# Small attentions with a written order of issue, layer 2's closing steps moved into the first of them, and a state scan over two states at a time

## The chip, the cores and the metric

The kernel runs on one core of a Trainium2 chip. The metric is the device time of one execution in microseconds (us). It computes a network of four layers over a batch of 16 sequences of 256 tokens with 128 features, all in float32.

The core has five engines that run their own instruction queues side by side, each strictly in order: TensorE (PE: matrix products and transposes, results in PSUM), VectorE (DVE), ScalarE (ACT), GpSimd (POOL) and SyncE (SP, which issues most of the DMAs). A queue whose next instruction waits for another engine holds back everything behind it.

## The reference, cut to what matters

Every layer adds an attention-like result times a gated second result to `x`, and normalises in between:

```python
xn = _layernorm(x)
s = _L2_attn_ref(xn, ...)          # state space scan ("mamba")
g = _silu(_L2_ffn_ref(xn, ...))    # 16 experts, each token takes 2
x = x + s * g
xn = _layernorm(x)
s = _L3_attn_ref(xn, ...)          # 16 heads with a penalty from gates
g = _silu(_L3_ffn_ref(xn, ...))    # two layers: local attention, gated MLP
x = x + s * g
```

The scan in layer 2, for each of 256 inner channels `d` and 16 states `n`, over the tokens of a sequence:

```python
dA = exp(dt_t[..., None] * A)
h = h * dA + (dt_t * u_t)[..., None] * B_t[:, None, :]
y = einsum('bdn,bn->bd', h, C_t)
```

The experts: `h = relu(x @ W1[e] + b1[e]); y = h @ W2[e] + b2[e]`, and a token's result is the sum over its two experts of gate times `y`. The local attention of layer 3: tokens shifted by one in half of the features, `qkv` projection, queries and keys divided by their lengths and rotated, 8 heads with 64 features, windows of 64 tokens that see themselves and the window before, softmax, output projection, added to its input. It is computed twice, each time followed by a gated MLP.

## The kernel before, in words

**Layout.** Tokens are held in 32 tiles of 128 partitions (tokens) by 128 features: `self.x`, the normalised `self.xn`, and `self.xnT`, its transpose. A sequence ("batch" b) is tiles 2b and 2b+1; a "chunk" c is four tiles.

**Layer 2's scan** (`attn2`). Channels lie on partitions (two halves h of 128), tokens in the free dimension, two sequences (512 tokens) to a group, so 8 groups. A step k is one state n of one half h of a group: 32 steps to a group, 256 in all. A step has: `decay` on ACT (`dab`, the exponential, L1122), `states` on DVE (a product `dbb` in PSUM, L1129, then the scan `st`, L1132), `outputs` (the product `hc` with C, L1143, on POOL, in some stretches on DVE) and `sums` on PE (an identity product that adds `hc` over the states into `py`, L1153). `decay` is issued 3 steps ahead, `sums` 3 behind. The rows B and C are loaded for each state, broadcast to all partitions (`bn`, `cn`, 256 KB each, by SP). Within the same steps lies the `prepare` of a later group (projections, convolution by taps, softplus of the step sizes: L1008 to L1086) and the end of an earlier one (`skip` L1159, `times` L1165, `project` L1173, `done` L1184).

**Layer 2's experts** (`ffn2`). After a router, the first 32 steps of the scan also send each token's row twice to a sorted place in DRAM (64 indirect DMAs on POOL, L1328). From step 34 on, 47 blocks of 256 sorted tokens go through their expert's two weights. A block is four "pieces", and `layer2` gives each piece a step by a list (`at`, filled by `later`); before, steps 14 and 15 of each 32 get none. The bias of the second product is one more product (`first` times a `b2` row, L1397). Results go to DRAM, one DMA for each block (L1412).

**Layer 2's end.** After the last piece, `bring` fetches a token tile's two results (2 indirect DMAs on POOL, L1448), `weigh` multiplies by the gates and adds (ACT L1458, DVE L1459), `gated_add` adds silu of that times `s` to `x` (L207 to L209), and `norm_tiles` normalises a chunk: statistics (L168, L169) on DVE, a power on POOL (L158, L159), the normalised tile (L172), transposes and a copy to `xnT` (L194, L195). Each has a step in the list, three quarters of a step per tile; while this runs, `hc` is done on DVE (`alone`). Everything in these steps is chained by `pin`, which fixes the order of issue on each engine to the order of the program.

**Layer 3.** `layer3` loads the weights, computes `gates3` (64 products with one column, L1485, two powers on POOL, L1490 and L1495, a transpose), then runs `local_attention`, `gated_mlp`, both again, and the last attention. `local_attention` is a pipeline written out by hand over i from -3 to 16, in which five batches are in different stages: `begin` (transposes, L1708, and copies to `hT`), `turned` (projection L1717, square on ACT L1730, length sums L1731, rotation L1732, L1735 on DVE, L1740 on POOL), `values` (L1747), `lengths` (reciprocal roots on DVE, L1664 to L1674, scaled keys L1760), `across` (transposes L1767), `scores` (mask L1778, products L1787, maxima L1797, exponentials L1806, shares L1814 and L1815), `keys_first` (L1825), `weigh` (L1839) and `finish` (L1855, L1862). It isn't pinned: a scheduler that orders instructions before the program is built may move them past each other.

Of the kernel before, what the change touches and what calls it, by code (L numbers as in the profile page):

```python
# [19 lines left out]
P = 128  # L20
B = 16
# [52 lines left out]
class Net:  # L74
# [756 lines left out]
    def layer2(self, ydram, consts):  # L831
# [10 lines left out]
        with ExitStack() as ctx:  # L842
            fin = ctx.enter_context(self.tc.tile_pool(name="l2_f", bufs=2))
# [18 lines left out]
            experts = self.ffn2(ctx, consts["experts"])  # L862


            k = SENT + 1
            later(k, experts["begin"])
            for i in range(experts["pieces"]):
                k += 1
                while k % 32 in (14, 15):
                    k += 1  # L870
# [3 lines left out]
            fetch = self.fetch = k + 2  # L874
            for t in range(NT):
                k = fetch + 3 * t // 4
                later(k, lambda t=t: experts["bring"](t))
                later(k + 3, lambda t=t: experts["weigh"](t, f))
                if t % 4 == 3:
                    c = t // 4  # L880
                    k = max(k + 4, STEPS + 11 if c == 7 else 0)
                    later(k, lambda c=c: self.gated_add(fin, 4 * c, chunk(f, c), 4))
                    later(k + 1, lambda c=c: self.norm_tiles(fin, psa, c, "pa"))

            mark = len(nc.cur_bb.bb.instructions)
            for k in range(max(at) + 1):
# [3 lines left out]
                scan["step"](k, k < SENT or k >= fetch)  # L890
                for f_ in at.get(k, ()):
                    f_()
            self.pin(mark)

# [15 lines left out]
    def layer2_constants(self, cp):  # L910
# [12 lines left out]

        first = cp.tile([P, P], F32, name="first")
        nc.gpsimd.memset(first, 0.0)
        nc.gpsimd.memset(first[0:1, :], 1.0)
# [17 lines left out]
        return {"scan": scan, "experts": (wr, br, b1, step, row, first)}  # L944

    def attn2(self, ctx, psa, consts, later):
# [12 lines left out]
        AHEAD, BEHIND = 3, 3  # L959
# [4 lines left out]
        dap, stp, hcp = enter("a2_da", AHEAD + 2), enter("a2_st", 3), enter("a2_hc", BEHIND + 2)  # L964
        bc = enter("a2_b", 4)
        dram = enter("a2_d", 2, space=DRAM)
        psd = enter("a2_db", 1, space=PSUM)
        psy = enter("a2_py", 1, space=PSUM)
# [7 lines left out]
        state = {}  # L976

        def prepare(gr, base):
# [109 lines left out]
            def broadcast(n):  # L1088
                for i, name in ((8, "bn"), (24, "cn")):
                    d[name, n] = self.load(  # L1090
                        bc, d["dr"][i + n, :].partition_broadcast(P), name, shape=[P, T]
                    )
# [54 lines left out]
        def sums(k):  # L1147
# [3 lines left out]
            if n == 0:  # L1151
                d["py", h] = psy.tile([P, T], F32, name=f"py{h}")
# [33 lines left out]
        def step(k, alone):  # L1186
# [7 lines left out]
            elif k == STEPS:  # L1194
                outputs(k - 1, None)
# [797 lines left out]
```

## Time and profile before

| what | value |
|---|---|
| median of 3 runs | 3000.88 us (2999.2 to 3001.28) |
| the profiled execution's own time | 3015.23 us |
| its span, first to last instruction | 3013.5 us |
| busy: PE, DVE, ACT, POOL | 2490.4, 2033.4, 1523.9, 1352.7 us |
| mean granted TensorE clock | 0.884 |

The span can be cut into stages by the first and last start of their lines: the scan's steps run from 874.0 (first L1129) to 1596.9 (last L1132), the sends from 910.6 to about 997, the experts from about 1014 to 1519, the fetches from 1524.6, the first small attention from about 1666 to 2026, the second to 2498, and the last attention to the end. "Busy" is the time in which an engine had at least one instruction running. PE's matrix products are pipelined and their ends are modelled, so that its busy share overstates it; for PE, times from one start to the next are the safer measure. Idle time of an engine that isn't the bottleneck costs nothing.

### The profile page before, as it was taken

How to read it: one execution, taken by the hardware profiler on the slowest of the kernel's cores; microseconds unless marked ns; L12 is line 12 of the kernel's file. 1: busy time of each engine (PE TensorE's matmuls, PEld its weight loads, DVE VectorE, ACT ScalarE, POOL GpSimd, SP SyncE). 2: the span in 40 equal slices, each digit the busy share in tenths (PEclk: the TensorE clock that was granted, in tenths of full speed). 3: DMA queues.
4: the chain of work that ended last, by engine and by line, in shares of the span. 5: the costliest groups of instructions: out<-in, count | busy, mean ns of one | idle time of the engine just before them, and what ended most of it. 6: DMA issues, size and time to landing. Idle time of an engine off the chain costs nothing.

```text
span 3013.5 us, 48937 instructions
## 1 busy us (share of the span) xinstructions
PE 2490.4 (83%) x17715; PEld 1618.9 (54%) x17743; DVE 2033.4 (67%) x4222; ACT 1523.9 (51%) x3371; POOL 1352.7 (45%) x1185
## 2 busy tenths in 40 slices
PE   5999983779666699999944699988799998789988
PEld 3666572556431366666613366665366665555555
DVE  4666423335488688888885678854678864478885
ACT  1555460213244466667641367771267774465564
POOL 2000002113237566665665545541355554288886
PEclk8999985779876799999975799998899999899998
DMA  2110002000113466666631000000100000112110
GB/s 64 29 30 26 8 4 100 1 15 15 43 46 120 132 186 178 181 180 179 183 100 53 14 14 13 16 8 0 39 15 12 15 12 4 36 39 45 31 47 8
DMA packets 155195, 168.94 MB, mean 56 GB/s; under 512 B 22817, under 2 KB 102874, under 8 KB 154954
## 3 DMA queue, kind: packets, MB, share of 16 engines
q1 hardware_dynamic: 146378, 147.71, 17.8%
q0 software_dynamic: 6496, 17.05, 1.7%
q8 instruction: 141, 2.31, 0.3%
q10 hardware_dynamic: 2080, 1.05, 0.1%
q14 instruction: 100, 0.82, 0.1%
HBM read 127.57 MB, written 29.79 MB: 52 GB/s over the span
## 4 chain that ended last, share of the span: by engine, by line
PE 27%; DVE 23%; POOL 8%; ACT 8%; issue 4%; DMA 2%; SPq 1%; another core or an unknown queue 0%; DVEq 0%; POOLq 0%; ACTq 0%
PE py L1153 5%; ACT p L1806 3%; POOL e L313 3%; DVE st L1132 2%; DVE rot L1732 2%; DVE ss L1731 2%; DVE sn L1735 2%; PE py L1399 2%; PE ph L1373 2%; DVE nm L1797 2%; PE ps L1787 2%; PE ph L1927 2%; PE pa L1008 1%; PE pa L325 1%; PE ph L1931 1%
## 5 line engine op out<-in xcount | busy, mean ns | idle before, releaser
L346 DVE TENSOR_REDUCE nmax<-pa 128x2 f32<-128x512 f32 x512 | 329.5, 683 | 142.4 <-PE pb L335 112.6
L335 PE MATMUL pb<-qa,kT 32*128 32x256 f32 x2048 | 387.3, 422 | 26.5 <-ACT e L356 26.5
L356 ACT ACTIVATE e<-pb 128x512 f32<-128x512 f32 x512 | 286.2, 594 | 228.4 <-PE pb L335 207.2
L325 PE MATMUL pa<-kT,qT 32*128 32x256 f32 x2048 | 367.1, 435 | 19.2 <-DMA kT<-qkd 17.7
L1143 POOL TENSOR_TENSOR hc<-st,cn 128x512 f32<-128x512 f32 x207 | 264.2, 1278 | 208.0 <-DVE dbb L1129 91.6
L1153 PE MATMUL py<-hc,ident 128*128 128x512 f32 x512 | 298.1, 674 | 65.6 <-DVE hc L1143 32.0
L1132 DVE TENSOR_TENSOR_SCAN st<-dab,dbb 128x512 f32<-128x512 f32 x256 | 312.5, 1221 | 34.1 <-ACT dab L1122 4.5
L325 PEld LDWEIGHTS pa<-kT,qT 32*128 32x128 f32 x2048 | 232.7, 200 | 103.3 <-issue 55.4
L335 PEld LDWEIGHTS pb<-qa,kT 32*128 32x128 f32 x2048 | 249.7, 195 | 55.4 <-ACT e L356 47.0
L1122 ACT ACTIVATE dab<-dl,A_log 128x512 f32<-128x512 f32 x256 | 181.3, 719 | 147.7 <-DVE st L1132 105.6
L313 POOL TENSOR_TENSOR e<-e,pen 128x1024 f32<-128x1024 f32 x96 | 228.9, 2395 | 59.1 <-ACT e L356 58.3
L1806 ACT ACTIVATE p<-ps,nm,rl 128x128 f32<-128x128 f32 x512 | 227.8, 466 | 29.8 <-DVE nm L1799 29.0
L1815 POOL TENSOR_TENSOR p<-p,den 128x512 f32<-128x512 f32 x128 | 133.0, 1041 | 231.4 <-DVE den L1814 225.8
L158 POOL TENSOR_SCALAR ln_r<-ln_mv 128x4 f32<-128x4 f32 x32 | 7.4, 232 | 495.3 <-DVE ln_st L168 419.4
L1717 PE MATMUL pm<-wqkv,hT 128*128 128x512 f32 x384 | 209.9, 661 | 17.7 <-DVE hT L1711 8.4
L1740 POOL TENSOR_TENSOR rot<-rot,sn 128x512 f32<-128x512 f32 x128 | 162.6, 1270 | 108.5 <-DVE sn L1735 61.9
L1129 DVE TENSOR_TENSOR dbb<-du,bn 128x512 f32<-128x512 f32 x256 | 202.9, 793 | 6.6 <-DMA bn<-dr 0.6
L1153 PEld LDWEIGHTS py<-hc,ident 128*128 128x128 f32 x512 | 95.2, 210 | 169.4 <-issue 76.8
L1730 ACT ACTIVATE sq<-pm 128x512 f32<-128x512 f32 x128 | 75.1, 618 | 136.2 <-PE pm L1717 136.2
L1787 PE MATMUL ps<-kT,qT 64*64 64x128 f32 x2048 | 136.1, 287 | 0.0
L382 PE MATMUL pm<-e,vaug 128*32 128x256 f32 x2048 | 128.9, 394 | 3.1 <-DVE s L416 3.1
L1787 PEld LDWEIGHTS ps<-kT,qT 64*64 64x64 f32 x2048 | 90.4, 136 | 72.1 <-issue 69.3
(375 smaller groups left out, 5614.2 us busy)
## 6 DMA issues: line engine op xcount, KB each, us to landing
bn<-dr SPq DMA_DIRECT2D x128, 256.0 KB
cn<-dr SPq DMA_DIRECT2D x128, 256.0 KB
w<-in_L_ffn_W_dram SPq DMA_DIRECT2D x94, 256.0 KB
qkd<-qk SPq DMA_DIRECT2D x32, 256.0 KB
v<-v SPq DMA_DIRECT2D x64, 128.0 KB
f_y<-y SPq DMA_DIRECT2D x47, 128.0 KB
f_x<-zero POOLq DMA_DIRECT2D x8, 704.0 KB
xr<-f_x SPq DMA_DIRECT2D x44, 128.0 KB
```

The costliest lines, as they stand in the source:

```text
L313: eng.tensor_mul(pairs[m], pairs[m], pen.to_broadcast([P, 2, 2, S]))
L325: nc.tensor.matmul(pa[:, t, :], qbuf[b % 4][r : r + 32, g, ts], kbuf[b % 4][r : r + 32, g, :], start=True, stop=True,)
L335: nc.tensor.matmul(pb[:, t, :], kbuf[b % 4][r : r + 32, g, ts], qas[m // 8][r : r + 32, g % 2, :], start=True, stop=True,)
L346: nc.vector.tensor_reduce(nbuf[n // 8 % 2][:, :, u // 4, u % 4, 8], pa, AX.X, ALU.max, negate=True)
L356: nc.scalar.activation(e, pb, AF.Exp, scale=scale)
L1129: mul = nc.vector.tensor_mul(db, d["du"][:, h, :], d["bn", n])
L1132: nc.vector.tensor_tensor_scan(d["st", r], d.pop(("da", r)), db, 0.0, ALU.mult, ALU.add)
L1143: ins = eng.tensor_mul(d["hc", r], d.pop(("st", r)), d["cn", r // 2])
L1153: nc.tensor.matmul(d["py", h], self.ident, d.pop(("hc", r)), start=(n == 0), stop=(n == N - 1))
L1717: nc.tensor.matmul(pj, hTs[b % 3][:, t * P : (t + 1) * P], d["qkv"][:, j * 512 : (j + 1) * 512], start=True, stop=True,)
L1787: nc.tensor.matmul(ps[i][64 * half : 64 * half + 64, c, w, :], qT[f, 2 * u + c, q0 : q0 + 64], kT[f, 2 * u + c, keys[half] : keys[half] + ...
L1806: nc.scalar.activation(p[:, c, w, :], ps[i][:, c, w, :], AF.Exp, scale=r[:, w, 0, h + 2 * c : h + 2 * c + 1], bias=nm[:, c, w : w + 1], ac ...
```

## The change

1. **The scan takes two states at a time.** `dab`, `dbb`, `st`, `hc`, `bn` and `cn` become tiles of 128 by 2 by 512. The multiply, the scan and the product each run once per pair of steps over 1024 elements; the exponential (its scale differs by state) and the sum on PE stay single. The first token of a sequence has its step size set to 1e28, so that a scan starts afresh there, and two states can lie end to end. Rings: `dab` 3 pairs, `st` 2, `hc` 3, `bn` and `cn` 2 (before: 5, 3, 5, 4 single). `decay` is 4 steps ahead, `sums` 5 behind. `dbb` takes two PSUM banks.
2. **Experts.** The bias of the second product moves out of the blocks: the gates' transpose `gT` and eight products with the biases (`spread`, `biases`, `biased`, in the first 32 steps) fill `f` beforehand, and `weigh` adds both results to it on DVE. Hidden results have one PSUM bank instead of two; transposes and second results share another. Six of each 32 steps get no piece before step 224, and from there on none is left out, which puts the last piece at step 261 (before: 237).
3. **Layer 2's end** leaves the pinned steps. `layer2` returns a function `end(n)`, which for tile n brings, for tile n-1 weighs, and for a chunk adds, takes statistics, or normalises. `local_attention` calls it seven times before its loop and twice in each round in its first run; its transposes in `begin` also fill `xnT`.
4. **Order of issue of `local_attention`.** `turned`, `values`, `scores`, `begin` and `finish` are split into their parts on PE, ACT, DVE and POOL, placed one by one in the loop, and the loop is pinned. Copies to `hT` and of the values move from DVE to ACT.
5. **`gates3`** comes after the first `local_attention`.

```diff
+            later(1, experts["spread"])
+            for c in range(NT // 4):
+                k = (4, 7, 16, 19, 22, 25, 28, 31)[c]
+                later(k, lambda c=c: experts["biases"](psa, c))
+                later(k + 1, lambda c=c: experts["biased"](c))
...
-                while k % 32 in (14, 15):
+                while k < STEPS - 32 and k % 32 in (5, 9, 12, 14, 15, 19):
...
+        def end(pool, n):
+            if 0 <= n < NT:
+                experts["bring"](pool, n)
+            if 0 <= n - 1 < NT:
+                experts["weigh"](n - 1)
+            c, r = divmod(n - 5, 4)
+            if 0 <= c < NT // 4 and r == 0:
+                self.gated_add(fin, 4 * c, chunk(f, c), 4)
+            if 0 <= c < NT // 4 and r == 1:
+                stats(c)
+            if 0 <= c < NT // 4 and r == 2:
+                normed(c)
...
-        AHEAD, BEHIND = 3, 3
+        AHEAD, BEHIND = 4, 5
...
-        dap, stp, hcp = enter("a2_da", AHEAD + 2), enter("a2_st", 3), enter("a2_hc", BEHIND + 2)
-        bc = enter("a2_b", 4)
+        dap, stp, hcp = enter("a2_da", 3), enter("a2_st", 2), enter("a2_hc", 3)
+        bc = enter("a2_b", 2)
...
-            db = psd.tile([P, T], F32, name="dbb")
-            mul = nc.vector.tensor_mul(db, d["du"][:, h, :], d["bn", n])
-            outputs(k - 1, mul)
-            d["st", r] = stp.tile([P, T], F32, name="st")
-            nc.vector.tensor_tensor_scan(d["st", r], d.pop(("da", r)), db, 0.0, ALU.mult, ALU.add)
+            db = banks["db"].tile([P, 2, T], F32, name="dbb")
+            du = d["du"][:, h, :].rearrange("p (o t) -> p o t", o=1).to_broadcast([P, 2, T])
+            mul = nc.vector.tensor_mul(db, du, d["bn", n])
+            outputs(k - 2, mul)
+            d["st", r] = stp.tile([P, 2, T], F32, name="st")
+            wide = lambda t: t.rearrange("p o t -> p (o t)")
+            nc.vector.tensor_tensor_scan(
+                wide(d["st", r]), wide(d.pop(("da", r))), wide(db), 0.0, ALU.mult, ALU.add
+            )
...
-            nc.tensor.matmul(py[:, q, :], first, b2s[j % 3], start=True, stop=False)
...
-        def weigh(t, f):
-            g0, g1 = (got.pop(("rows", t, k)) for k in range(K))
-            nc.scalar.activation(f[:, t, :], g0, AF.Copy, scale=gate[:, 0, t : t + 1])
-            nc.vector.scalar_tensor_tensor(
-                f[:, t, :], g1, gate[:, 1, t : t + 1], f[:, t, :], ALU.mult, ALU.add
-            )
+        def weigh(t):
+            for k in range(K):
+                nc.vector.scalar_tensor_tensor(
+                    f[:, t, :], got.pop(("rows", t, k)), gate[:, k, t : t + 1], f[:, t, :],
+                    ALU.mult, ALU.add,
+                )
...
                     if l == 0:
+                        with tc.tile_pool(name="l2_g", bufs=3) as got:
+                            self.local_attention(X, d, lambda n: end(got, n))
                         g, dr = self.gates3(gp, dram)
-                    self.local_attention(X, d)
+                    else:
+                        self.local_attention(X, d)
...
-                hT = hTs[b % 3]
-                nc.vector.tensor_copy(hT[0:64, :], pt[0:64, :])
-                nc.vector.tensor_copy(hT[64:128, 1:S], pt[64:128, 0 : S - 1])
+            def begun(b):
+                pt, hT = rows[b].pop("pt"), hTs[b % 3]
+                nc.scalar.copy(hT[0:64, :], pt[0:64, :])
+                nc.scalar.copy(hT[64:128, 1:S], pt[64:128, 0 : S - 1])
+                if end is not None:
+                    nc.scalar.copy(self.xnT[:, b * S : (b + 1) * S], pt)
...
+            mark = len(nc.cur_bb.bb.instructions)
+            if end is not None:
+                for n in range(7):
+                    end(n)
             for i in range(-3, B + 1):
                 run(scores, i, 0)
-                run(turned, i + 2, 0, 0)
-                run(turned, i + 2, 0, 1)
-                run(keys_first, i - 1, 2)
+                run(times, i + 2, 0, 0)
+                run(squares, i + 2, 0, 0)
+                run(powers, i, 0, 0)
+                run(times, i + 2, 0, 1)
+                run(squares, i + 2, 0, 1)
+                run(turned, i + 2, 0, 0)
+                run(keys_first, i - 1, 2)
+                run(powers, i, 0, 1)
+                run(shares, i, 0, 0)
+                run(turned, i + 2, 0, 1)
                 run(keys_first, i - 1, 3)
+                run(shares, i, 0, 1)
...
+                if end is not None:
+                    end(2 * i + 13)
                 run(scores, i, 1)
...
+                if end is not None:
+                    end(2 * i + 14)
+                run(begin, i + 3)
+                run(begun, i + 3)
                 run(weigh, i, 1)
-                run(begin, i + 3)
+            self.pin(mark)
```

## The prediction

> **What bounds the kernel now.** I read the table of stretches first, having cut the span at the places where the code changes stage. Its columns are the stretch, its length, then busy time (and instructions) of PE, PEld, DVE, ACT and POOL, granted clock, DMA share and GB/s.
>
> ```profile
> 1014.00:1519.00 505.00, 479.20 (x2115) 311.45 (x2114) 443.76 (x438) 337.33 (x605) 306.81 (x241) 0.98 0.61 176
> 1519.00:1673.00 154.00, 59.07 (x158) 33.50 (x159) 95.11 (x220) 38.68 (x71) 94.75 (x92) 0.61 0.23 66
> 1673.00:2022.00 349.00, 317.25 (x2787) 206.40 (x2800) 268.38 (x734) 238.02 (x764) 178.41 (x163) 0.95 0.06 13
> 2022.00:2141.00 119.00, 98.30 (x465) 64.90 (x462) 53.41 (x148) 19.53 (x30) 23.37 (x32) 0.84 0.02 7
> 2157.00:2500.00 343.00, 314.43 (x2829) 207.85 (x2840) 257.63 (x708) 238.22 (x765) 174.85 (x160) 0.96 0.06 13
> ```
>
> In order: scan with experts, layer 2's end, first small attention, its gated layer, second small attention. The scan has two full engines (PE 479 and DVE 444 of 505). Layer 2's end has none: PE is busy for 59 of 154 us. In the attentions PE is busy for nine tenths.
>
> Next the timeline of the scan, and three single rows (start, duration, engine, line, operation).
>
> ```profile
> 1512.71 1.22 DVE L1132 TENSOR_TENSOR_SCAN st<-dab,dbb 128x512 f32<-128x512 f32 x1
> 1512.72 1.27 POOL L1143 TENSOR_TENSOR hc<-st,cn 128x512 f32<-128x512 f32 x1 [0.83 <-DVE dbb L1129]
> 1513.96 0.70 DVE L1129 TENSOR_TENSOR dbb<-du,bn 128x512 f32<-128x512 f32 x1
> ...
> 1499.86 1.27 POOL L1165 TENSOR_TENSOR xz<-xz 128x512 f32<-128x512 f32 x1
> 1499.88 1.80 DVE L1129 TENSOR_TENSOR dbb<-du,bn 128x512 f32<-128x512 f32 x1
> ...
> 887.41 2.28 DVE L719 TENSOR_TENSOR_SCAN f_run<-ones,f_num 128x1024 f32<-128x1024 f32 x1
> 898.14 1.22 DVE L1275 TENSOR_TENSOR f_run<-f_run,f_num 128x1024 f32<-128x1024 f32 x1
> ```
>
> A step is multiply, a gap of 0.12, scan: 2.09 us. Twice the width costs 2.28 and 1.22, not 2.44 and 1.40. A multiply beside a POOL operation grows to 1.80.
>
> Last, layer 2's end (timeline and chain of waits) and the steady attention (waits: total, times, longest).
>
> ```profile
> 1602.18 1.14 POOL L1448 DMA_INDIRECT got<-f_y,slot  x1 [0.19 <-issue]
> 1603.63 0.96 POOL L1448 DMA_INDIRECT got<-f_y,slot  x1 [0.30 <-issue]
> ...
> 1618.46 2.11 DVE L208 TENSOR_TENSOR gate<-gate,s 128x512 f32<-128x512 f32 x1 [0.70 <-ACT gate L207]
> ...
> 1635.28 10.37 PE pc L1485 x48
> 1658.97 5.44 POOL g L1490
> 1666.99 5.45 POOL reach L1495
> ...
> PE ps L1778 <- DVE rl_t L1673: 9.7, 10, 1.0
> ```
>
> 64 gathers go one by one on POOL, about 1.26 us apart, and every chunk of four tiles passes gather, addition, layernorm, transpose before the next moves on; then come the gates. The attention's first work on DVE (L1731) starts at 1673.65. From there PE repeats every 20.38 us (L1855 at 1864.86 and 1885.24), with waits of 1.0 us and some 0.4 in small ones: 18.9 us of PE per batch.
>
> **The Trainium skill.** (1) "VectorE: DVE Perf Modes", section on the TRN2 errata: a fp32 tensor_tensor takes (N+151)/0.96 ns, so the fixed part is paid once per instruction; 512 gives 691, 1024 gives 1224. The trace agrees (0.70 and 1.22). (2) "SBUF — State Buffer", "SBUF: two separate sides": a DVE operation with two SBUF inputs and a GpSimd operation take a lock, and the later one waits for the whole of the other. The 1.80 above and the 2.11 of L208 (0.69 elsewhere) agree. (3) "ScalarE: Activation LUTs", "What ACT_TABLE_LOAD costs": 1283 ns and a drain of 1380. The trace has the 1283; at 1541.73 the next activation followed after 1.29, so I take 1.28 and keep 2.66 as the upper end.
>
> **The change, part by part.**
>
> *Scan in pairs.* Per pair DVE runs one multiply (1.22), the gap (0.12) and one scan (2.28). POOL's product, 128x1024, takes 2.35 (L1078's row) and starts with the scan, so it ends some 0.1 after it, and the next multiply must wait for that: 3.75 per pair, 1.88 per step against 2.09. Each group of 32 steps adds 5.6 us of DVE (L1070, L1081, L1159 twice, L1184): 0.18 per step; waiting for other POOL work makes the mean multiply 0.825 instead of 0.70: 0.12. DVE falls from 2.39 to 2.18 per step, to 0.91.
> PE per step before: the sum 0.86 (start to start in the timeline); experts 30 pieces in 32 steps, four to a block, a block being hidden 2×0.87, result 2×0.90, bias 2×0.22, transposes 0.44: 1.04; a group's preparation and projection, 14×0.86 plus 2.3, over 32: 0.45. Sum 2.35, of 2.51 measured (175 scans in 440 us). After: bias matmuls gone, 26 pieces in 32: 0.86+0.81+0.45 = 2.12, to 0.90. The 32 steps from 224 have a piece each and no preparation: 1.91.
> I take both down together: 2.51×0.907 = 2.28. Where does it start? The 64 sends on POOL end at 997 and the experts' tokens wait for them, so a faster start of the scan waits at step 32: nothing gained before 1014 (step 38). Then 186×2.28 + 32×2.04 + 6 steps of pieces alone at an estimated 1.5 = 498: the last result is stored at 1512, with the scan finished; before it was 1519 with 16 steps left. ACT rises to about 1.8 per step, still under 2.28. Broadcast loads halve in number and double in size, issued five steps ahead; eight bias loads replace 47 on SP; nothing waits there. Tighter buffers (two state pairs, one bank for hidden) bound the pace: 2.13 if none shows, 2.51 if they eat the gain.
>
> *Layer 2's end.* Before: 1519 to 1673.65, 154.6 us. After, what must precede the attention: store to first gather 5.4 (as 1519.14 to 1524.57), 14 gathers of seven tiles 17.6 (addition and statistics of chunk 0 run beneath them), POOL's power 1.3, normalising 1.3, transposes, copies, projection and square 3.2: 28.8. L1731's successor starts at 1541, 132.6 earlier. The layer's weights load on SP behind the last store, under these 29 us (before, SP issued them in 10.6, from 1648.86 to 1659.44); if late they cost up to 5.
>
> *First attention.* What was moved lands here, per batch (two tiles): DVE +3.2 (four weighings at 0.3, half an addition 0.7, statistics 0.8, normalising 0.5), minus the value and hT copies 2.2, plus 0.5 for locks: 16.8 becomes 18.3. ACT 14.7 + 2.2 for those copies, xnT and silu + 1.3 table loads: 18.2 (19.6 with the drain). POOL 11.0 + four gathers 5.0 + 0.65: 16.7. All are under PE's 18.9 but close, and order of issue is fixed: a weighing that waits for its gather holds up DVE's score maxima behind it, which ACT's exponentials and then PE wait for. A gather has half a batch (10 us) of lead over its use, on a POOL with 4 us free. I take 20.9 per batch (19.3 to 23): +8 over 16.
>
> *Gates.* They now stand between attention and gated layer, and the order shows them in PE, DVE and POOL ahead of its first chunk: 64 products 12.2, power 5.4, power 5.4 partly beside statistics: +22 (15 to 26). In the old place they were part of the 154.6.
>
> *Second attention.* No moved work; DVE 15, ACT 16.6; the fixed order can at most close PE's 1.5 us of waits per batch. I take half, 19.7: −11 (19.0 to 20.6).
>
> Sum: −132.6 + 8 + 22 − 11 = −114 against the profiled execution's 3015.2 (span 3013.5, 1.7 around it), which ran 0.5% above the median 3000.9. Predicted median: 2888.
>
> **Rivals.** *The scan keeps 2.5 per step*: a POOL extra (2.9 us for L1084, 2.5 for two L1165) delays the product, two state pairs give only the multiply's 1.2 us of slack, and DVE stops. For it: 307 of 505 us on POOL and locks both ways. Against: PE and DVE both lose a tenth. +58: 2946. *Everything closes up*: 2.13 per step (−28), 19.3 and 19.0 per batch (−26, −11): 2823. For it: no engine's load exceeds these; against: four engines over 85%. *Slower*: gathers on POOL fall behind products and additions, DVE waits at each weighing, twice per batch, and a fixed order lets nothing pass. It decides from 20.4+(114+8)/16 = 28 us per batch, which is 3.5 us of wait at each weighing beyond my 20.9; at 30 the time is 3034. Against: POOL has 4 us to spare per batch. *The pin repeats what the scheduler did*: second attention unchanged, 2899; inside my case.
>
> **How the numbers follow.** Mine 62%, scan unchanged 16%, all closes 14%, slower 4%, other losses that stay faster 3%, a tie 1%. Range 2830 to 2948: from near the closed case to just over the unchanged scan. What this measurement can tell from no change is 0.2%, 6 us: faster 0.95, same 0.01, slower 0.04.
>
> **What would show it.** Scans of 2.28 every 4.5 us; last store near 1512; first L1803 within 30 us of it; batches of 20 to 21 us, then 19 to 20; 20 us of PE near idle after the first attention. A first attention over 25 us per batch, or scan pairs of 5 us, would make it wrong.

## The result, and the profile after

| | before | after |
|---|---|---|
| median of 11 runs on the same chips | 3000.47 us (2994.54 to 3002.32) | 2976.30 us (2966.43 to 2988.81) |
| ratio, 95% interval | | 0.9923 [0.9904, 0.9941] |
| the profiled execution | 3015.23 us | 2966.91 us |

The change makes the kernel faster by 24 us, well outside 0.2%. The forecast was 2888, and 2976 lies above its range. The two profiled executions differ by 48 us, since the one before ran 15 us above its median and the one after 9 below its own. The eleven runs after spread over 22 us, and the shortest has the higher mean granted clock (0.897, against 0.889 in the longest). The stages below are cut from profiles and add up to 48, not 24.

The table of stretches of the kernel after, cut at its own stages: scan with experts, layer 2's start-up before the attention, first small attention, gates with the first gated layer, second small attention. Columns as before: stretch, length, busy time of PE, PEld, DVE, ACT, POOL, granted clock, DMA share, GB/s.

```profile
1014.00:1522.00 508.00, 464.25 (x1941) 289.03 (x1939) 436.38 (x250) 335.69 (x607) 310.11 (x146) 0.99 0.57 179
1522.00:1551.00 29.00, 4.74 (x21) 3.13 (x20) 11.31 (x39) 3.41 (x7) 19.46 (x25) 0.62 0.42 123
1551.00:1955.00 404.00, 317.27 (x2848) 206.61 (x2847) 314.17 (x819) 284.60 (x865) 234.91 (x221) 0.89 0.08 19
1955.00:2086.00 131.00, 103.58 (x478) 71.06 (x478) 53.94 (x154) 17.73 (x25) 34.50 (x38) 0.79 0.00 1
2086.00:2454.00 368.00, 292.08 (x2852) 192.81 (x2851) 254.93 (x681) 258.32 (x833) 178.04 (x162) 0.96 0.08 19
```

The 154 us in which no engine was full have become 29. But the first attention, with the same 317 us of PE as before, takes 404 instead of 349 us, and DVE has gone from 268 to 314 us in it.

| stage, us | before | forecast | after |
|---|---|---|---|
| last expert result stored at | 1519.1 | 1512 | 1522.4 |
| from there to the attention's first work on DVE (L1731, L1803) | 154.6 | 29 | 29.2 |
| first small attention, to its last sum into `X` | 352.7 | 361 | 403.4 |
| gates (now here) and first gated layer | 111.3 | 133 | 131.3 |
| second small attention | 360.5 | 350 | 367.3 |
| the rest | 515.3 | 515 | 511.7 |

A steady batch is the distance between two sums into `X`: 20.4 us before in both attentions; after, 24.1 and 23.7 in turn (mean 23.9) in the first and 20.9 in the second.

Who waits for whom. First the list of waits of DVE in the first attention of the kernel after (1640 to 1850), then the list of PE's and DVE's waits in its second (2150 to 2370); columns: waiting line, what ended the wait, us in total, times, longest.

```profile
DVE gate L208 <- ACT gate L207: 17.0, 5, 4.6
DVE nm L1867 <- PE ps L1858: 5.8, 5, 1.4
```

```profile
DVE nm L1867 <- PE ps L1858: 41.8, 21, 3.9
PEld po L1916 <- ACT oT L1926: 27.0, 21, 1.7
PE po L1916 <- ACT oT L1926: 16.1, 21, 0.9
```

In the second attention DVE is early: it waits 42 us in 220 for scores. In the first that reserve is gone. What used it up is in the groups of DVE in the first attention (count, busy us and mean ns, idle before):

```profile
L1518 DVE SCALAR_TENSOR_TENSOR xnT<-got,gates,xnT 128x128 f32<-128x128 f32 x30 | 22.1, 736 | 0.5
L904 DVE TENSOR_SCALAR xn<-x,ln_mv,ln_r 128x128 f32<-128x128 f32 x16 | 7.3, 516 | 0.0
L208 DVE TENSOR_TENSOR gate<-gate,s 128x512 f32<-128x512 f32 x5 | 3.5, 692 | 17.0 <-ACT gate L207 17.0
```

A weighing costs 736 ns on the mean where the shortest of the 64 takes 320, and each product with the gate has 3.4 us of idle DVE ahead of it. One such place, from the timelines of ACT and of DVE:

```profile
1734.44 0.37 ACT L1926 COPY oT<-po 128x256 f32<-128x256 f32 x1 [0.28 <-PE po L1916]
1734.83 1.28 ACT L207 ACT_TABLE_LOAD   x1
1736.12 0.63 ACT L207 ACTIVATE gate<-xnT 128x512 f32<-128x512 f32 x1
...
1739.08 1.28 ACT L1881 ACT_TABLE_LOAD   x1 [1.42 <-DVE nm L1869]
```

```profile
1732.08 1.62 DVE L1518 SCALAR_TENSOR_TENSOR xnT<-got,gates,xnT 128x128 f32<-128x128 f32 x2
1736.78 0.69 DVE L208 TENSOR_TENSOR gate<-gate,s 128x512 f32<-128x512 f32 x1 [3.09 <-ACT gate L207]
```

ACT issues the silu behind its copies, the last of which has waited for PE, and must load a table for it; DVE stands at L208 for 3.1 us, with the maxima (L1867) queued behind it, and ACT's exponentials then wait 1.4 us for those maxima. It looks like a complete story: a wait that the fixed order passes on. The experiments show that it is only a part.

### The profile page after: what moved, and what is told of

Its sections match the earlier page's. It is cut to its first block, busy times and chain, and to the rows that moved or that the text cites. A ratio compares the mean times of both kernels' runs of the same rounds, so it can differ in the third digit from the quotient of the medians.

```text
span 2965.2 us, 47535 instructions
## 1 busy us (share of the span) xinstructions
PE 2391.3 (81%) x17543; PEld 1561.1 (53%) x17543; DVE 1984.8 (67%) x3841; ACT 1559.5 (53%) x3490; POOL 1360.3 (46%) x1084
## 3 DMA queue, kind: packets, MB, share of 16 engines
q8 instruction: 139, 2.28, 0.3%
## 4 chain that ended last, share of the span: by engine, by line
PE 24%; DVE 15%; ACT 14%; POOL 8%; issue 3%; DMA 3%; SPq 1%; POOLq 0%; DVEq 0%; ACTq 0%
ACT p L1881 6%; PE py L1192 3%; POOL e L313 3%; DVE nm L1867 2%; PE ps L1858 2%; PE ph L2035 2%; ACT pT L1907 1%; PE po L1916 1%; PE ph L1435 1%; PE pa L1037 1%; PE ph L2039 1%; PE pa L325 1%; PE py L2051 1%; DMA xr<-f_x 1%; PE pb L335 1%
## 5 line engine op out<-in xcount | busy, mean ns | idle before, releaser
L1182 POOL TENSOR_TENSOR hc<-st,cn 128x1024 f32<-128x1024 f32 x111 | 261.2, 2353 | 194.6 <-DVE dbb L1165 117.1
L1169 DVE TENSOR_TENSOR_SCAN st<-dab,dbb 128x1024 f32<-128x1024 f32 x128 | 292.7, 2287 | 24.5 <-ACT dab L1155 9.1
L1192 PE MATMUL py<-hc,ident 128*128 128x512 f32 x512 | 267.7, 613 | 10.3 <-DVE hc L1182 8.7
L1165 DVE TENSOR_TENSOR dbb<-du,bn 128x1024 f32<-128x1024 f32 x128 | 188.8, 1475 | 5.0 <-DMA bn<-dr 2.4
L1867 DVE TENSOR_REDUCE nm<-ps 128x4 f32<-128x512 f32 x128 | 87.6, 684 | 107.8 <-PE ps L1858 106.5
L1916 PE MATMUL po<-pT,v 128*64 128x64 f32 (+1 forms) x1536 | 95.3, 265 | 64.2 <-ACT oT L1926 49.6
L1916 PEld LDWEIGHTS po<-pT,v 128*64 128x64 f32 x1536 | 76.5, 150 | 109.6 <-ACT oT L1926 83.0
```

The lines of the kernel that those rows point to most:

```text
L1165: mul = nc.vector.tensor_mul(db, du, d["bn", n])
L1169: nc.vector.tensor_tensor_scan(wide(d["st", r]), wide(d.pop(("da", r))), wide(db), 0.0, ALU.mult, ALU.add)
L1182: ins = eng.tensor_mul(d["hc", r], d.pop(("st", r)), d["cn", r // 4 * 2])
L1192: nc.tensor.matmul(d["py", h], self.ident, d["hc", r - r % 2][:, r % 2, :], start=(n == 0), stop=(n == N - 1))
L1916: nc.tensor.matmul(po[64 * i : 64 * i + 64, P * w + q0 : P * w + q0 + n], v[:, k, hs], pT[:, i, w, q0 : q0 + n], start=True, stop=True, ti ...
```

## The experiments

The stages of all runs, in us, as in the table above (start-up, first attention, gates and gated layer, second attention), and the ratio to the kernel before on the same chip:

| run | start-up | first | gated | second | ratio [95%] |
|---|---|---|---|---|---|
| before | 154.6 | 352.7 | 111.3 | 360.5 | 1 |
| after | 29.2 | 403.4 | 131.3 | 367.3 | 0.9923 [0.9904, 0.9941] |
| e_split | 30.3 | 422.9 | 133.5 | 371.3 | 0.9994 [0.9981, 1.0007] |
| e_copy | 29.8 | 401.1 | 131.3 | 375.1 | 0.9924 [0.9899, 0.9949] |
| e_nopin | 42.8 | 393.8 | 130.5 | 350.7 | 0.9864 [0.9827, 0.9901] |
| e_old1 | 29.3 | 409.3 | 131.3 | 360.2 | 0.9874 [0.9847, 0.9900] |
| e_endfirst | 111.4 | 366.6 | 133.0 | 370.7 | one run |
| e_chunkfirst | 30.1 | 372.8 | 130.7 | 367.9 | one run |
| e_nogather | 9.7 | 405.1 | 131.3 | 378.3 | one run |
| e_anchor | 29.2 | 436.0 | 130.8 | 351.1 | 0.9974 [0.9959, 0.9988] |
| e_slots | 33.1 | 399.3 | 130.6 | 378.4 | 0.9861 [0.9829, 0.9892] |
| e_best | 33.3 | 394.1 | 130.7 | 351.1 | 0.9815 [0.9795, 0.9835] |
| e_best_gates | 33.0 | 396.9 | 111.2 | 371.5 | 0.9794 [0.9763, 0.9826] |
| e_scan | 33.1 | 398.0 | 130.6 | 350.9 | 0.9798 [0.9773, 0.9823] |
| e_final | 35.7 | 424.0 | 131.3 | 350.8 | 0.9905 [0.9882, 0.9929] |
| e_act | 33.0 | 414.8 | 130.6 | 350.9 | 0.9912 [0.9879, 0.9945] |

### The gate in two pieces (e_split)

```diff
             if 0 <= c < NT // 4 and r == 0:
-                self.gated_add(fin, 4 * c, chunk(f, c), 4)
+                at["gate", c] = g = fin.tile([P, 4, D], F32, name="gate")
+                nc.scalar.activation(g, chunk(f, c), AF.Silu)
             if 0 <= c < NT // 4 and r == 1:
+                ...  # product, sum into x
                 stats(c)
```

> Layer 2's gate in two pieces: silu in the place where the whole gated addition stood, product and sum one call of end() later (half a batch), beside the statistics. Both table loads stay. First theory (DVE stands in fixed order behind a silu that ACT issues only after the copies of oT, 3.1 to 4.6 us each time, 8 times): the rounds with a chunk's addition fall from 26.4 to about 22.5 us, the first attention from 403 to about 372, the whole by 25 to 35. Rival (ACT's two table loads of 1.28 us are the cost, wherever DVE stands): ACT is late for the exponentials all the same, the first attention stays above 393. Rival (any fixed order costs this): stays at 403.

The wait at the gate is gone, and the first attention is 20 us longer: rounds of 24.5 and 26.6. My first theory fell. Product, sum and statistics now form one lump of DVE work at the start of a round. From 1640 to 1850, PE's products wait 19.8 us, in five times, for DVE (L1842, released by `den`, L1898). That the lump costs more than the wait did is a likely reading; no run takes the two apart.

### No table loads (e_copy)

```diff
             if 0 <= c < NT // 4 and r == 0:
-                self.gated_add(fin, 4 * c, chunk(f, c), 4)
+                ...
+                nc.scalar.copy(g, chunk(f, c))
+                ...  # product, sum into x
```

> silu left out of layer 2's closing addition (a plain copy in its place), so that no table is loaded within the first attention; the order is that of the changed kernel, so DVE still waits for ACT's copy behind the copies of oT. First theory (DVE's place in the order): DVE's wait falls only by the load, from 3.1-4.6 to 1.8-3.3 us, and the exponentials' own reload of 1.28 goes too: 8 x 1.3 to 2.6 = 10 to 21 us less, first attention at 382 to 393. Rival (table loads are the cost): rounds with an addition come down to the 21.4 us of the others, first attention at 363 to 370.

The silu is left out, and a plain copy stands in its place. 401.1 against 403.4: fourteen table loads of 1.28 us, 18 us of ACT (68 loads in the kernel after, 54 here), were worth about 2 us. Neither theory's number came. DVE still stood ahead of the product, 12.3 us in five times.

### No chain (e_nopin), and the old second attention (e_old1)

```diff
-            self.pin(mark)
```

> local_attention without its chain (pin), everything else as in the changed kernel: the scheduler may move instructions past each other in both small attentions. Theory of the fixed order (it costs 7 us in the second attention and part of the 44 in the first): the second attention goes from 363 back to about 356 or below, the first to below 385. Rival (the moved work costs the same whoever orders it; the written order is no worse): the second stays at 360 to 366 and the first at 395 to 410, or grows where the scheduler hoists gated additions ahead of the maxima.

> The second small attention alone in the form of the kernel before (no chain, copies to hT and of the values on DVE), the first as in the changed kernel. If the written order or the copies on ACT cost the second attention its 7 us: it goes from 362.7 to 354-358 and the whole falls by about 7. If the 7 us came from what lies around it (its weights, the clock): it stays at 360-366.

Both second attentions are shorter than the chained one. With the pieces and the copies on ACT, but no chain, it takes 350.7, with rounds of 20.4 and last rounds of 16.2, 13.2 and 8.4 where the chain had 20.8, 20.3 and 10.1. The old form gives 360.2, as before. So the pieces gain about 10 us and the chain loses 17 or more, most of it in the last three rounds (51 us for 38). Within the steady rounds, what goes is PE's wait for the single `po` bank: 16.1 us in 220 with the chain for the products (the 27.0 of the weight loads run in part at the same time and don't add to it). In the second attention of the run without the chain, the products' largest wait is another, and the weight loads' wait for the bank is small:

```profile
PE ps L1849 <- ACT p L1881: 12.7, 11, 1.2
PEld po L1916 <- ACT oT L1926: 4.7, 11, 0.4
```

In the first attention the scheduler drew fetches and additions forward: three rounds of 33.4, 29.3 and 29.2, then 20.4 in the rest. Start-up and attention together take 436.6, against 432.6 with the chain: not faster there, only in the second attention.

### Which part of the moved work (e_endfirst, e_chunkfirst, e_nogather)

```diff
# e_endfirst
-                for n in range(7):
+                for n in range(NT + 8):
                     end(n)
...
-                if end is not None:
-                    end(2 * i + 13)
...
-                if end is not None:
-                    end(2 * i + 14)
# e_chunkfirst: gated_add, stats, normed of all chunks ahead of the loop
# e_nogather: the weighings read one constant tile
-                nc.gpsimd.indirect_dma_start(...)
+                gk = xs_
```

> All of layer 2's end (64 fetches, weighings, additions, statistics, normalising) ahead of the first attention's loop, none within it; the loop's chain is unchanged. If the moved work makes the loop's rounds longer (23.9 us per batch): they fall to the second attention's 20.9, the first attention to about 360, and the stretch from the last store to the attention's first work on DVE grows from 29 to about 95 (50 more fetches at 1.26 and the last chunk's end). Rival (the chain, or the copies to xnT, or the clock after a long idle stretch, make the first attention slow by themselves): rounds stay above 22.5.

> Additions, statistics and normalising of all chunks run ahead of the loop, on what f holds then (so the values are others: the fetched rows come too late for them); fetches and weighings stay in the loop. It cuts the moved work in two. Theory A (DVE's and ACT's part of a chunk: silu, product, sum, statistics, normalising, about 2.2 us of DVE per batch): rounds fall from 23.9 to 21 to 21.7. Theory B (fetches on POOL, the weighings behind them and their locks): they stay at 23 to 23.9. Both in part: about 22.4.

> The 64 fetches left out: the weighings read one constant tile, so that POOL has 5 us less per batch and no weighing waits for a transfer or a fetch's lock; all of DVE's and ACT's work stays in its place. Theory A (DVE's and ACT's part): rounds stay at 23 to 23.9. Theory B (fetches): they fall to 21 to 21.7. The stretch before the attention falls from 29 to about 12 either way.

These three agree, each in a single run. With nothing moved into it, the loop runs at 20.9 to 22.4, mostly 20.9. Without additions, statistics and normalising: 21.4, 21.4, 22.0 in turn, mean 21.6. Without the fetches: 23.7 to 24.2 as in the kernel after, once the first rounds are past. In the rounds whose granted clock is 1.00 throughout, the three stand at 20.9, 21.4 and 24.1. So of the 3 us per batch, some 2.3 to 2.7 belong to the work that is done once per chunk on DVE and ACT, 0.5 to 0.7 to weighings with fetches, and the fetches on POOL cost nothing that shows. (In e_chunkfirst the scheduler drew seven of the eight chunks' additions forward into the scan, whose last store moved to 1539.9; its loop is what counts here.) DVE's waits for the maxima, in e_chunkfirst (1640 to 1800) and in e_nogather (1640 to 1830):

```profile
DVE nm L1867 <- PE ps L1858: 17.6, 7, 3.0
```

```profile
DVE gate L208 <- ACT gate L207: 14.6, 4, 4.6
DVE nm L1864 <- PE ps L1855: 5.3, 4, 1.9
```

Without the chunk's work part of DVE's reserve is back; without the fetches it isn't.

### Held in place without a chain (e_anchor)

Each instruction of `end` is tied behind the one ahead of it on its engine; the attention's own are free.

> No chain over the loop; only the instructions of layer 2's end are held behind the instruction ahead of them on their engine in the program, so that the scheduler orders the attention's own work freely but can't draw the moved work forward, as it did in the run without a chain (33, 29, 29 us in the first three rounds). If the chain's 0.5 us per round and its slow end (12 us) are the attention's own and the moved work costs 3 us per batch wherever it is spread: second attention 351 as without a chain, first about 385, the whole at 2940 to 2955. Rival (the moved work's cost grows again without the chain): first attention at 394 or more, the whole not under 2960.

The rival was right, and more than right: 436.0, with rounds of 26 to 31. What makes it worse was not taken apart. The second attention, where nothing is tied, takes 351.1 again.

### Other places for the moved work (e_slots), and a free second attention (e_best)

```diff
...
+            elif part == "mid":          # ahead of the middle maxima
+                c, r = divmod(i + 3, 2)
+                if r == 0 and c < NT // 4:
+                    normed(c)
+                if r == 1 and c + 1 < NT // 4:
+                    added(c + 1)         # product, sum, statistics
+                for t in (12, 13):
+                    weigh(2 * i + t)
+                bring(2 * i + 14)
+            else:                        # end of the round
+                ...
+                    silu(c)              # half a round before its product
+                bring(2 * i + 15)
...
# e_best besides
-            self.pin(mark)
+            if end is not None:
+                self.pin(mark)
```

> Layer 2's moved work takes other places in the same chain. In the undisturbed rounds DVE waits for scores twice: 3.9 us ahead of the maxima in the middle of a round, 0.3 ahead of those at its start. All of DVE's moved work (both weighings, product, sum, statistics, normalising: about 3.6 us per batch) goes ahead of the middle maxima; the silu is issued half a round before its product, so that DVE never waits for it. If the place decides (one us of DVE ahead of the early maxima lengthens the round by one us, ahead of the middle ones by nothing until 3.9 are used): rounds fall from 23.9 to 21 to 21.6, the first attention to 368-378, the whole from 2976 to about 2945-2955. Rival (DVE's amount decides, wherever it stands): rounds stay at 23 or more, the first attention over 395.

> As the run with the moved work ahead of the middle maxima, and the chain only in the first small attention: the second is left to the scheduler, with the pieces as they are. Expected: both gains add, first attention 368-378, second 351 in place of 367, the whole 2928 to 2940. Rival: the second attention without a chain was fast only because the first had none either: stays at 360 or more.

The place helps far less than I expected, and the rival was the nearer: rounds of 24.1 and 22.3, a mean of 23.2 for 23.9, and a first attention of 399.3. In e_best the second part held: 351.1 in the second attention, and 0.9815 [0.9795, 0.9835] in all. Why the place gave so little can be read in e_best. All the weighings there cost 346 ns, but now the first operation in the slot pays. The group of the four normalisings between 1756 and 1761 (min/median/max), and POOL's timeline beside it:

```profile
L904 DVE TENSOR_SCALAR xn<-x,ln_mv,ln_r x4: 335/338/2571, 1756.7 to 1759.7; 128x128 f32<-128x128 f32 x4
```

```profile
1755.91 1.05 POOL L1922 TENSOR_TENSOR p<-p,den 128x512 f32<-128x512 f32 x1
1756.91 1.27 POOL L1839 TENSOR_TENSOR rot<-rot,sn 128x512 f32<-128x512 f32 x1
1758.13 1.04 POOL L1922 TENSOR_TENSOR p<-p,den 128x512 f32<-128x512 f32 x1
```

The first normalising starts at 1756.7 and ends only when POOL's last product does, at 1759.2: 2.57 us for 0.34. In the same place product and sum cost 1.50 and 1.41 instead of 0.69. This fits the lock that the Trainium skill, page "SBUF — State Buffer", section "SBUF: two separate sides", describes: it is taken for a whole instruction. The attention's large DVE operations that read an operand from PSUM keep their time (L1804: 0.68 us on the mean in both attentions); the work that was moved in has all its operands in SBUF, and met the lock in both arrangements.

An estimate from the means and shortest times: weighings and normalisings lose 2.0 us per batch in the kernel after (4 x 0.42 + 2 x 0.18), and normalisings, product and sum 2.1 in e_best (2 x 0.65 + 0.77). So these waits did not go, they moved to other operations. With them, DVE is busy for 191.06 of the 210 us from 1640 to 1850 in e_best, or 21.1 us of each round of 23.2. That is more than the whole undisturbed round of 20.9, so at these durations the work doesn't fit into such a round in any order.

### The gates elsewhere (e_best_gates)

```diff
-                        g, dr = self.gates3(gp, dram)
                     else:
+                        g, dr = self.gates3(gp, dram)
                         self.local_attention(X, d)
```

> As the run before it, with gates3 after the first gated layer, ahead of the second attention. If the gates' 20 us are one serial chain (products, power, power) with nothing beside it: the stretch from the first attention to the end of its gated layer falls from 131 to about 111, and the second attention grows by 5 to 20, since in POOL's order both powers stand ahead of its first sums: the whole falls by 0 to 15. Rival (the gates' 20 us follow them wherever they stand): no change in the sum.

The 20 us move as a block: gated layer 131 to 111, second attention 351 to 371. The rival was right. POOL there:

```profile
2081.74 5.42 POOL L1577 TENSOR_TENSOR g<-base,g 128x32 f32<-128x32 f32 x1 [27.61 <-DVE g L1576]
2087.23 0.12 POOL L1580 MEMSET base<- 128x32 f32 x1
2088.14 5.44 POOL L1582 TENSOR_TENSOR reach<-base,reach 128x32 f32<-128x32 f32 x1 [0.79 <-DVE both L1584]
```

### The scan's preparation one step later (e_scan)

```diff
-            parts += [(21, size), (21, small), (22, plus), (23, rest), (23, log), (24, exact)]
-            parts += [(25, delta), (26, inputs)]
+            parts += [(21, size), (21, small), (22, plus), (24, rest), (24, log), (25, exact)]
+            parts += [(26, delta), (26, inputs)]
```

> As the run with the moved work ahead of the middle maxima and no chain in the second attention, and in the preparation of a later group (softplus of the step sizes) DVE's two steps go one step later each, so that they stand behind a scan of 2.29 us and not ahead of it: before, DVE waited 36 us for ACT's and POOL's parts of that chain within the 426 us from 1014 on (19 in the kernel of before). If DVE's in-order waits set the pairs' pace (2.34 per step against the forecast 2.28): these waits fall under 10 us, the last result is stored at 1503 to 1512 in place of 1521 to 1530, and the whole falls by about 10 to 15. Rival (the experts' pieces, PE and their transfers set it): the waits move to other lines and the last store stays at 1518 to 1530.

DVE's waits from 1014 to 1440, first in the kernel after, then in e_scan:

```profile
DVE du L1099 <- ACT u L1096: 21.9, 6, 3.9
DVE dl L1110 <- POOL u L1107: 14.5, 6, 2.5
DVE st L1169 <- ACT dab L1155: 9.1, 6, 1.5
DVE dbb L1165 <- DMA bn<-dr: 2.4, 4, 1.5
```

```profile
DVE dbb L1192 <- DMA bn<-dr: 21.3, 9, 4.5
DVE st L1196 <- ACT dab L1182: 9.2, 6, 1.5
```

The 36 us are gone, and 21 came back as waits for the broadcast rows, which are loaded from what that preparation ends with. The last store is at 1516.1, against 1520.7 in e_best; in e_final and e_act, which have the same scan, it is at 1522.0 and 1523.0. The runs whose scan is that of the kernel after lie between 1518 and 1532, so no gain can be told from their spread; the ratio, 0.9798, is e_best's within the intervals.

### Normalising on ACT (e_final, e_act)

```diff
-                nc.vector.tensor_scalar(
-                    self.xn[:, t, :], self.x[:, t, :], mv[:, j, 0:1], r[:, j : j + 1], ALU.subtract, ALU.mult
-                )
+                nc.scalar.activation(
+                    self.xn[:, t, :], self.x[:, t, :], AF.Identity, scale=r[:, j : j + 1], bias=m[:, j : j + 1]
+                )
```

> As the run before it; besides, layer 2's normalising (4 x 0.96 us on DVE per chunk with its waits beside POOL) goes to ACT as a scaled copy with a bias, and the statistics to the round after the addition, so that DVE has 4.3 and 3.2 us of moved work in alternate rounds in place of 5.9 and 4.7. If DVE's load with its locks sets the first attention's rounds (24.1 and 22.3): rounds fall to 21.2 to 22.2, the first attention from 394 to 372-382, the whole by 12 to 22. Rival (ACT, now at 18.8 of 22 us per batch, takes DVE's place; or PE's lower clock holds the rounds): rounds stay over 22.7 on average.

> As the run with the later softplus steps; layer 2's normalising goes from DVE to ACT, but half a round earlier than on DVE, so that the transposes of the next batch don't wait for it as they did in the run that put it right ahead of them (rounds of 28.5). Addition and statistics stay together ahead of the middle maxima. If DVE's load sets the rounds: those in which DVE normalised fall from 22.3 to 20.9, those with an addition stay at 24.1; first attention from 395 to 385-390, the whole by 5 to 10. Rival (ACT's load): the 22.3 stay or grow, first attention not below 394..

Both are slower than e_scan, and both rivals' numbers came. In e_final rounds of about 28.5 alternate with rounds of 20.5 to 20.9: the round with DVE's addition has become as short as one without moved work, and the other waits for the normalised tile, which ACT makes directly ahead of PE's transposes. In e_act that wait is gone and another is there: ACT stands for the factor from DVE and POOL (L903) and its copies to `hT` come late. PE's longest waits from 1640 to 1830, in e_final and in e_act:

```profile
PE pm L1804 <- ACT xn L906: 14.8, 4, 3.7
```

```profile
PE pm L1815 <- ACT hT L1809: 11.1, 8, 2.6
```

So DVE's amount isn't the whole cause either. PE's clock, the other rival that e_final named, is not what holds the rounds with an addition. These are two rounds of the kernel after (columns as in the table of stretches); the longer one has the full clock throughout:

```profile
1646.85:1670.54 23.69, 19.82 (x176) 12.90 (x175) 21.49 (x59) 16.65 (x54) 15.92 (x16) 0.86 0.09 23
1670.54:1694.61 24.07, 18.50 (x184) 12.21 (x183) 19.62 (x50) 19.44 (x57) 15.73 (x15) 1.00 0.10 23
```

In e_best, too, the rounds of 24.1 come at mean clocks of 0.86, 0.93 and 1.00 alike. For the rounds of 23.7, all of which have a clock near 0.86, it isn't shown. What remains open is how the 2.3 us or more per batch divide between DVE's time, its locks, and the waits at the gate. No version was found in which the moved work costs under 2.3 us per batch in the loop (e_slots and e_best: 23.2 against 20.9); a chain for the first attention made around it from the start wasn't tried. Nor does a run take the paired scan or the moved bias out alone, so that their own worth isn't known.

## Why the prediction was wrong

The direction was right, and so was the largest term. Against the forecast sum of −114 the two profiles show −48, a miss of 66, and it lies in these steps:

- **Layer 2's end, "28.8"**: 29.2 measured. The fetches of the first tiles, one by one on POOL, and the short chain behind them set it. Right.
- **The scan, "at 1512"**: 1522.4, a miss of 10; 1516 to 1532 in the other runs in which nothing was drawn into the scan. Undisturbed pairs run as worked out:

```profile
1489.07 2.29 DVE L1169 TENSOR_TENSOR_SCAN st<-dab,dbb 128x1024 f32<-128x1024 f32 x1
1489.17 2.35 POOL L1182 TENSOR_TENSOR hc<-st,cn 128x1024 f32<-128x1024 f32 x1 [1.40 <-PE py L1192]
1491.39 1.23 DVE L1165 TENSOR_TENSOR dbb<-du,bn 128x1024 f32<-128x1024 f32 x1
1492.76 2.29 DVE L1169 TENSOR_TENSOR_SCAN st<-dab,dbb 128x1024 f32<-128x1024 f32 x1
```

  3.69 per pair. From 1014 to 1440 there were 90 scans, or 2.37 us per step, for 2.28. The mean multiply there was 1.53 us for an assumed 1.46, and DVE waited 36 us for the preparation's other engines, for 19 before. The term "waiting for other POOL work" held only the multiply's part of that. But e_scan took those waits away, and from step 38 to step 224 its steps still came at 2.35 us, for 2.38 in the kernel after and 2.37 and 2.38 in e_final and e_act, which have e_scan's scan. What sets the pace stays open. The start was right in part: in the timeline of the scan step 32 came 21 us earlier than before (982 for 1003), and a third of this lead was lost up to step 38, which came at 1010.5 where the prediction had 1014. The 1.91 for the last 32 steps doesn't follow from the prediction's own prices (0.86 for the sum and 1.00 for a piece are 1.86), which is worth 2 us over them.
- **First attention, "I take 20.9 per batch"**: 23.9 measured, 403.4 in all, a miss of 43 us. **This is the step that failed.** The sum for DVE was 18.3 per batch. Its own work there is 16.1 now (169.28 us of 220 at 20.9 in the second attention), not 14.6; each weighing took 0.74, not 0.3, and a normalising 0.52, not the 0.26 behind the 0.5 per batch; and 1.7 per batch went into standing at the gate, which I had not priced. With statistics, product and sum as measured that is 16.1 + 2.9 + 2.6 + 1.7 = 23.3 of 23.9. (The parts overlap a little: counted in one, DVE was busy for 178.96 of the 210 us from 1640 to 1850, 20.4 per round, or 22.1 with the gate.) I had compared loads with PE's 18.9 and called them close. DVE's load was mis-sized, and in a fixed order its reserve also lies in places: 3.9 us ahead of the middle maxima, 0.3 at the start of a round. That the place is only a small part, e_slots shows: 0.7 us per round. The mechanism that I had named (a weighing waits for its fetch) wasn't the one: e_nogather leaves the rounds as they are.
- **Gates, "+22"**: 20.0. Right, and e_best_gates moves just that.
- **Second attention, "the fixed order can at most close PE's 1.5 us of waits"**: it lost 7 where I had 11 of gain, a miss of 18. The order written by hand made new waits: PE's products waited 34.5 us in 220 (16.1 of them for the `po` bank), for 11.7 in the kernel before (2200 to 2420). Its steady rounds are 20.9 for 20.4, and it did not close up the last rounds. What I took for a bound from above was none from below. The split pieces alone did give the gain (350.7).
- The rest of the miss against the median is the two profiles' distance from their medians: I had taken 13 off for that of before, and the median after lies 9 above its profile.

Of the rivals, "everything closes up" was furthest off. "The scan keeps 2.5" gave the nearest time, for a wrong reason. That the change makes it faster was right. Neither sign of being wrong showed, a first attention over 25 us per batch or pairs of 5 us: both were set too wide for a sum of many terms.

## What to carry to other kernels

Work that is moved under a full stage must be priced with what it meets there, not at its shortest time. Here a weighing took 0.74 us for 0.32, and when the weighings had found a quieter place, the normalising took 0.98 for 0.34 in their stead. List also where the stage's engine waits in the undisturbed round, and for how long, and what is queued behind the new work; but first see whether the new load, waits included, fits into the round at all. Here a written order of issue paid, if anything, only where it held work that the scheduler would draw forward: 432.6 us for start-up and first attention against 436.6 without it, one profile each. Over the second attention, which had no such work, it cost 17 us, and taking it away there was the one edit that gave a gain without a loss. When one wait is removed and the time grows, as in e_split, that wait was not the cost by itself: take the whole moved work out, then its halves, before mending single waits.

## What the runs showed of the hardware that was not expected

- A DVE operation on 128x128 whose operands are all in SBUF took 2.57 us instead of 0.34 beside a row of POOL products, through all of them. In e_best from 1640 to 1850, four of the five first normalisings of a chunk did so (2.57 to 2.94 us, until the third of three POOL instructions had ended, each of which begins in the trace before the one ahead of it is over). The fifth, at 1848.70, ended after 1.11 us, with the first of two. So the lock can pass between such POOL instructions, but mostly didn't; what decides is not known.
- The Trainium skill, "ScalarE: Activation LUTs", "What ACT_TABLE_LOAD costs", has a drain of 1380 ns beside the load. Here the activation follows 1.29 us after the load's start (1734.83 to 1736.12), so no drain shows, and leaving fourteen loads out gained 2 us of that stage.
- The chained second attention varied from 367 to 378 us between seven runs of the same code, and the granted clock goes with it. Rounds of 20.9 us have a clock of 1.00, those of 21.6 to 22.5 one of 0.92. Three rounds of e_slots, columns as in the table of stretches:

```profile
2154.76:2175.67 20.91, 17.21 (x178) 11.69 (x179) 15.86 (x44) 15.94 (x53) 11.11 (x10) 1.00 0.06 14
2175.67:2197.27 21.60, 18.55 (x178) 12.17 (x179) 15.87 (x44) 16.03 (x53) 11.09 (x10) 0.92 0.06 14
2197.27:2219.70 22.43, 18.56 (x178) 12.60 (x179) 15.89 (x44) 15.94 (x53) 11.09 (x10) 0.92 0.06 14
```

  Of the engines only PE is busy for longer in the second and third. The 0.92 is one stretch of 3.41 us at half the clock. Of their first twelve rounds 0, 2, 3, 2, 5, 10 and 9 are such ones in the kernel after, e_chunkfirst, e_endfirst, e_split, e_copy, e_nogather and e_slots, at 367.3, 367.9, 370.7, 371.3, 375.1, 378.3 and 378.4 us. In 30 of these 31 rounds the first start on DVE, ACT or POOL that is over 0.06 us off its place in an undisturbed round comes after the clock has fallen: the clock falls first, and the delay follows.
- The free second attention took 350.7 to 351.1 us in six runs, with a clock of 1.00 in each of those twelve rounds. Short waits of PE are not enough to bring the clock down: the chained one of the kernel after has 34.5 us of them in 220, none over 0.9, at 1.00, and the second attention of the kernel before has 11.7 in 220 at 0.97. What brings it down stays open.
